# Cross attention on one core: the last batch's right sums for product 4 placed ahead of block 12, and the first loads cut into smaller transfers

## The chip, the core and the metric

The kernel runs on one core of one Trainium2 chip. A core has five engines that run their own instruction streams side by side: TensorE (PE in the profile; its weight loads are listed apart as PEld), VectorE (DVE), ScalarE (ACT), GpSimd (POOL) and SyncE (SP), and 16 DMA engines that move data between HBM and the on-chip memory. SP, ACT and POOL can issue DMA transfers; "SPq" and "ACTq" in a profile row mean such an issue. The metric is device microseconds of one execution. Lower is better.

## The reference

There are 8 batches. All data are float32.

```python
q = jnp.einsum('bcn,dc->bnd', x1, Wq) + bq
k = jnp.einsum('bcn,dc->bdn', x2, Wk) + bk[:, None]
v = jnp.einsum('bcn,dc->bdn', x2, Wv) + bv[:, None]
attn = jax.nn.softmax(jnp.einsum('bnd,bdm->bnm', q, k), axis=2)
attn_out = jnp.einsum('bcm,bnm->bcn', v, attn)
return attn_out + x1
```

x1 and x2 are 8 x 512 x 1024 (batch, channel, position), Wq and Wk are 64 x 512, Wv is 512 x 512.

## The kernel before

The value projection is moved behind the attention. For each batch the kernel makes scores from queries and keys, takes exponentials e (positions m of x2 on the partitions, positions n of x1 along the row), forms y = x2 e, scales each column n by one over the sum of its exponentials, multiplies Wv y, and adds the bias and x1.

Both large products, y = x2 e (the first stage, banks ya and yc) and Wv y (the second stage, banks oa and oc), are cut into 2 x 2 blocks and done with seven block products in place of eight, in the manner of Strassen and Winograd. The table `MULT` (L298) names the operands of each: left blocks and left sums (S1 to S4, made from blocks of x2 or of Wv) and right blocks and right sums (T1 to T4, made from blocks of e or of y). Result block 12 comes out of product 3, block 22 out of 7 and 5, block 21 out of 4 and 6 on top of the bank of 7, block 11 out of 1 and 2. In the last batch products 2, 3, 4 and 7 of the first stage are themselves cut once more into seven products of half the size. `inner_left` (L349) and `inner_right` (L358) make the four left and four right sums for this; `multiply_onto` (L422) runs the seven half-size products, copies partial results from PSUM with ACT into tiles d and v, and `complete` (L450 to L453) adds v onto d on DVE.

`multiply_3` (L475) returns `evict`, called `evict_3`: `complete` (one DVE addition, L452), then two DVE additions (L483) that write block 12 of y from bank a and d. `multiply_4` (L456) starts with the half-size product 1, which needs blocks of e and x2 alone; its second step, half-size product 7, needs T3, one of the sums of `inner_right(s, 4, s.t["T4"], "eT2")`. These sums appear in the profile as eI4eT at L367, four additions of 128 x 512. `evict_y` (L490) has two steps: step 1 adds a PSUM bank and a partial result (L502), step 2 multiplies with one over the sum (L505, L507). `evict_o` (L509) adds bias and x1 to a block of the result and stores it; in the last batch its DVE work is at L526, L534 and L538.

The order on each engine is the order of the program: the whole kernel runs under `manual_schedule`, and nothing reorders it. `head` (L609) prepares batch 0, and `period(s, n, nn, nnn)` (L708) does the products of batch s with the scores of batch n between them. In the last batch n is None: no work of another batch stands between its products. Batches 2 to 5 and the last take the branch `seven`, in which product 7 is cut further too; of these only the last has no next batch.

In `head`, ten warm-up products of 128 x 128 (L635) run on TensorE while the first data come. ACT issues one transfer of Wq and Wk together (`wqk`, 256 KB, L630). SP issues, in this order: x1's channel tiles 0 and 1, then 2 and 3, of columns 0 to 511 (half 0; 512 KB each, L623); eight transfers of x2, 256 KB each (L644), the left 256 columns of each half for the four channel tiles and then the right ones; half 1 of x1 (L623); four blocks of x2 transposed (`load_a`, L133); Wv (L99). TensorE takes the queries of half 0 (L586, 8 products), the left keys (L601, tile ps_kc), the first tile of the right keys (ps_ka), and then the first scores.

Transfers of the hardware queues take their completion semaphores in turn from a ring of eight, common to SP and ACT. A transfer that comes after eight others waits on its issuing engine until the one eight before it has landed.

Of the kernel before, what the change touches and what calls it, by code (L numbers as in the profile page):

```python
# [15 lines left out]
def kernel(  # L16
# [47 lines left out]
    nc = tc.nc  # L64
    P = 128
    B, C, N = x1.shape
    D = wqk.shape[3]
    CT = C // P
    H = 512
# [16 lines left out]
    wqk_sb = const.tile([P, 2, CT, D], F32, name="wqk_sb")  # L86
# [9 lines left out]
    def load_values():  # L96
        for r in range(2):
            for k in range(2):
                nc.sync.dma_start(w[f"{r + 1}{k + 1}"], wvT[r, k])  # L99
# [28 lines left out]
    def load_a(s, *ks):  # L128
        for k in ks:
            s.a[k] = sb.tile(  # L130
                [P, MH, C // 2], F32, tag=f"a{k}", name=f"a{k}_{s.b}", bufs=1 + (k[0] == "2")
            )
            nc.sync.dma_start(s.a[k], x2T[s.b, int(k[0]) - 1, int(k[1]) - 1])  # L133
# [79 lines left out]
    def fold_halves(s, h, op):  # L213
        f = s.mx[h]
        nc.vector.tensor_tensor(f[:, 0, :], f[:, 0, :], f[:, 1, :], op)  # L215

    def highest(s, h, halves=True):
        if halves:
            fold_halves(s, h, ALU.max)
        s.top[h] = sb.tile([P, H], F32, tag="top", name=f"top_{s.b}_{h}", bufs=2)  # L220
        nc.gpsimd.partition_all_reduce(s.top[h], s.mx[h][:, 0, :], P, ReduceOp.max)  # L221
# [136 lines left out]
    def inner_right(s, i, x, *tags):  # L358

        v = {  # L360
            f"{q + 1}{r + 1}": x[:, ts(q, MH // 2), ts(r, H // 2)] for q in range(2) for r in range(2)
        }
        shape = [P, 4 // len(tags), MH // 2, H // 2]
        sums = [sb.tile(shape, F32, tag=t, name=f"eI{i}{t}_{s.b}") for t in tags]
        for z, (k, x, y, op) in enumerate(RIGHT):
            v[k] = sums[z // shape[1]][:, z % shape[1]]
            nc.vector.tensor_tensor(v[k], v[x], v[y], op)  # L367
        s.inner[i, "t"] = v
# [206 lines left out]
    def head_queries(s, x_sb, h, bank=None):  # L575


        if bank:
            ps = ps_a.tile([P, H], F32, tag=bank, name=f"ps_q_{s.b}_{h}")
        else:  # L580
            ps = ps_s.tile([P, 2, H], F32, tag="sc", name=f"ps_q_{s.b}_{h}")[:, 0, :]

        def add(*tiles):
            for c in tiles:
                for r in (lo, hi):
                    nc.tensor.matmul(  # L586
                        ps[r, :], wq_sb[:, c, :], x_sb[:, c, ts(h, H)], start=(c == 0), stop=(c == CT - 1)
                    )
            if c == CT - 1:
                nc.scalar.activation(s.q[:, ts(h, H)], ps, AF.Identity, bias=bq_sb)  # L590

        return add

    def head_keys(s, n, bank):

        ps = ps_a.tile([P, H], F32, tag=bank, name=f"ps_k{bank}_{s.b}")

        def add(*tiles):
            for c in tiles:
                for h, r in ((0, lo), (1, hi)):  # L600
                    nc.tensor.matmul(  # L601
                        ps[r, n], wk_sb[:, c, :], s.x[:, c, ts(h, H)][:, n], start=(c == 0), stop=(c == CT - 1)
                    )
            if c == CT - 1:
                nc.scalar.activation(s.k[:, n], ps[:, n], AF.Identity, bias=bk_sb)

        return add

    def head(s):  # L609

        s.q = sb.tile([P, N], F32, tag="q", name=f"q_{s.b}", bufs=2)
        s.k = sb.tile([P, H], F32, tag="k", name=f"k_{s.b}", bufs=2)
        x1_sb = sb.tile([P, CT, N], F32, tag="x", name="x1_head")
        x2_sb = sb.tile([P, 2, MH, H], F32, tag="e1", name="x2_head")
        s.x = x2_sb.rearrange("p a (b t) n -> p (a b) (t n)", t=2)  # L620

        def load_x1(c, h):
            nc.sync.dma_start(  # L623
                x1_sb[:, c : c + 2, ts(h, H)],
                x1[s.b, c * P : (c + 2) * P, ts(h, H)].rearrange("(t p) n -> p t n", p=P),
            )

        nc.gpsimd.dma_start(bqk_sb, bqk)
        nc.gpsimd.dma_start(bv_sb, bv)
        nc.scalar.dma_start(wqk_sb, wqk)  # L630
        warm = const.tile([P, P], F32, name="warm")
        nc.vector.memset(warm, 0.0)
        ps = ps_a.tile([P, H], F32, tag="a0", name="ps_warm")
        for _ in range(WARM):
            nc.tensor.matmul(ps[:, 0:P], warm, warm, start=True, stop=True)  # L635
        load_x1(0, 0)
        load_x1(2, 0)
        for n in HALVES:
            for c in range(CT):
                to, of = (  # L640
                    x.rearrange("p (h n) -> p h n", h=2)[:, :, n]
                    for x in (s.x[:, c, :], x2[s.b, ts(c, P), :])
                )
                nc.sync.dma_start(to, of)  # L644
        nc.scalar.activation(warm[:, 0:1], warm[:, 0:1], AF.Exp)
        load_x1(0, 1)
        load_x1(2, 1)
        load_a(s, "21", "22", "11", "12")
        load_values()
        tiles = range(CT)  # L650
        head_queries(s, x1_sb, 0, "c1")(*tiles)
        head_keys(s, left, "c0")(*tiles)
        more_keys = head_keys(s, right, "a0")
        more_keys(0)
        s.mx[0] = f = sb.tile([P, 2, H], F32, tag="fold", name=f"max_{s.b}_0", bufs=2)
        copies = [scores(s, 0, i) for i in range(2)]
        for g in range(2):
            nc.scalar.copy(s.e[0][:, g, 0, :], copies[0].ps[g])
            nc.vector.tensor_tensor(f[:, g, :], s.e[0][:, g, 0, :], copies[1].ps[g], ALU.max)
        fold_halves(s, 0, ALU.max)  # L660
        more_keys(*tiles[1:])
        copies[1]()
        more_queries = head_queries(s, x1_sb, 1)
        more_queries(0)
        for i, bank in ((2, "a"), (3, "c")):
            copy = scores(s, 0, i, bank)
            for g in range(2):
                nc.vector.tensor_tensor(f[:, 0, :], f[:, 0, :], copy.ps[g], ALU.max)
            copy()
        highest(s, 0, halves=False)  # L670
        sum_a(s, "S1", "S2")
        more_queries(*tiles[1:])
        load_x(states[1], x1)
        copies = [scores(s, 1, 0), scores(s, 1, 1), scores(s, 1, 2, "c")]
        for g in range(2):
            for i in range(MH):
                first_exponentials(s, g, i)
        for copy in copies:
            copy()
        fold(s, 0, 1, "sum", ALU.add)  # L680
        fold(s, 0, 2, "sum", ALU.add)
        fold(s, 1, 1, "max", ALU.max)
        fold(s, 0, 3, "sum", ALU.add)
# [24 lines left out]
    def period(s, n, nn, nnn):  # L708
# [54 lines left out]
        def add_exponential(i):  # L763
            exponential(n, 0, i)
            add_tile(n, 0, i)
# [20 lines left out]
        if seven:  # L786
            hooks = [{}, {}]
            if n:
                for i in range(MH):
                    lower(n, 0, i)  # L790
                hooks = [
                    {
                        1: lambda: copy_first(n, 0),
                        6: lambda: add_exponential(1),
                        5: lambda: add_exponential(2),
                    },
                    {6: lambda: add_exponential(3)},
                ]
            first(5, (lambda: exponential(n, 0, 0)) if n else None)
            inner_right(s, 3, s.t["22"], "eT1")  # L800
            inner_left(s, 4, s.a["22"], "a12")
            add_7 = multiply_7(s, hooks[0])
            add_7()
            evict_3 = multiply_3(s, hooks[1])
            evict_y(s, "22", (1,))
            evict_3()
            inner_right(s, 4, s.t["T4"], "eT2")
        else:
            first(5)
            if s.b == 0:  # L810
                inner_right(s, 3, s.t["22"], "eT1")
                for i in range(MH):
                    lower(n, 0, i)
            else:
                for i in range(MH):
                    exponentials(n, 0, i)
                start_sum(n, 0)
                inner_right(s, 3, s.t["22"], "eT1")
            first(7)
            if s.b > 1:  # L820
                inner_right(s, 4, s.t["T4"], "eT2")
            evict_3 = multiply_3(s, {})
            if s.b:
                evict_y(s, "22", (1,))
                evict_3()
            else:
                evict_3()
                evict_y(s, "22", (1,))
# [105 lines left out]
```

## Time and profile before

| what | value |
|---|---|
| median of 3 runs | 693.46 us (693.18 to 695.86) |
| profiled execution | 693.62 us |
| its span, first to last instruction | 691.8 us |
| PE busy | 682.8 us, 99% of the span |
| DVE busy | 628.9 us, 91% |
| ACT busy | 276.1 us, 40% |
| POOL busy | 193.5 us, 28% |
| share of the chain that ended last | PE 93%, DMA 3%, DVE 1%, SP's queue 1%, ACT 1% |
| granted TensorE clock | 1.000 |
| transfers issued by SP for x_head (x1, x2 of batch 0) | 4 of 512 KB, 8 of 256 KB; 6.3 and 6.5 us from issue to landing (median) |

In a row of a timeline the first number is the start in us from the span's start, the second the length, then come engine, line, operation, and the tiles as out<-in; a bracket at the end tells how long the engine stood idle before and what released it. A matmul row counts several passes of one instruction, and their ends are modelled. In a row of the chain that ended last, the numbers are start and length of a step that the end of the run hung on.

### The profile page before, as it was taken

What the parts mean: (1) busy time and instruction counts of PE and PEld (TensorE: products, weight loads), DVE (VectorE), ACT (ScalarE), POOL (GpSimd) and SP (SyncE); (2) the same over time, 40 slices, a digit from 0 to 9 for tenths busy, and PEclk for the clock granted to TensorE, in tenths of its full rate; (3) what the DMA queues carried; (4) which work ended last, traced back from release to release, by engine and by line L of the source; (5) the groups of instructions that cost most, each with busy time, mean ns of one, the idle gap of its engine ahead of it and who ended that gap; (6) DMA issues with size and microseconds to landing.
All of it is one profiled execution on the core that took longest, in us unless ns stands there. A gap on an engine that the chain in (4) does not pass through costs nothing.

```text
span 691.8 us, 6647 instructions
## 1 busy us (share of the span) xinstructions
PE 682.8 (99%) x2248; PEld 364.2 (53%) x2248; DVE 628.9 (91%) x809; ACT 276.1 (40%) x439; POOL 193.5 (28%) x147
## 2 busy tenths in 40 slices
PE   9999999999999999999999999999999999999997
PEld 5333554535545565455644566454754545545753
DVE  1999999988999889998999989999799988999785
ACT  2733353146233552345432454424544245243220
POOL 0123113522423223242142321623223232323000
PEclk9999999999999999999999999999999999999999
DMA  9676256954569754786628867198642864268303
GB/s 304 258 214 238 65 182 130 255 161 79 183 114 235 199 106 153 150 231 181 135 111 180 230 181 187 42 198 215 167 92 38 207 166 76 62 148 223 87 0 122
DMA packets 44723, 109.05 MB, mean 158 GB/s; under 512 B 4880, under 2 KB 7184, under 8 KB 44688
## 3 DMA queue, kind: packets, MB, share of 16 engines
q1 hardware_dynamic: 25856, 70.13, 30.1%
q0 software_dynamic: 17424, 36.25, 29.7%
q10 hardware_dynamic: 1408, 2.23, 1.0%
q8 instruction: 18, 0.29, 0.2%
q14 instruction: 17, 0.14, 0.1%
HBM read 72.62 MB, written 16.81 MB: 129 GB/s over the span
## 4 chain that ended last, share of the span: by engine, by line
PE 93%; DMA 3%; DVE 1%; SPq 1%; ACT 1%; issue 0%; DVEq 0%
PE ps_ya L321 24%; PE ps_i L374 17%; PE ps_oa L321 16%; PE ps_oc L321 12%; PE ps_s L191 6%; PE ps_yc L374 5%; PE ps_q L149 4%; PE ps_k L149 3%; PE ps_yc L321 3%; PE ps_ya L374 3%; DMA a<-in_x2T_dram 1%; DMA x_in_x_dram<-in_x_dram 1%; DMA x_head<-in_x_dram 1%; PE ps_sc L191 1%; PE ps_sa L191 1%; DVE aS L110 0%
## 5 line engine op out<-in xcount | busy, mean ns | idle before, releaser
L321 PE MATMUL ps_ya<-eT,aS 128*128 128x512 f32 x256 | 113.1, 595 | 0.0
L332 ACT COPY uy<-ps_ya 128x512 f32<-128x512 f32 x48 | 28.1, 588 | 139.6 <-PE ps_ya L321 126.7
L249 DVE TENSOR_TENSOR e<-e,top 128x1024 f32<-128x1024 f32 x60 | 70.5, 1228 | 11.0 <-POOL top L221 11.0
L321 PEld LDWEIGHTS ps_ya<-eT,aS 128*128 128x128 f32 x256 | 48.0, 190 | 60.9 <-issue 58.5
L253 ACT ACTIVATE e<-e 128x1024 f32<-128x1024 f32 x60 | 62.9, 1059 | 38.6 <-DVE e L249 37.1
L221 POOL PARTITION_ALL_REDUCE top<-max x16 | 32.8, 2052 | 150.8 <-DVE max L215 78.9
L226 POOL PARTITION_ALL_REDUCE den<-sum x16 | 63.4, 3961 | 40.8 <-DVE sum L215 35.8
L321 PE MATMUL ps_oa<-yT,w_S 128*128 128x512 f32 x128 | 57.6, 593 | 0.0
L321 PE MATMUL ps_oc<-y,w 128*128 128x512 f32 x128 | 57.6, 593 | 0.0
L321 PE MATMUL ps_ya<-e,a 128*128 128x512 f32 x128 | 56.3, 593 | 0.3 <-ACT e L244 0.3
L200 ACT COPY e<-ps_s 128x1024 f32<-128x1024 f32 x46 | 45.7, 1027 | 19.3 <-PE ps_s L191 17.5
L332 ACT COPY uo<-ps_oa 128x512 f32<-128x512 f32 x48 | 27.6, 584 | 54.2 <-PE ps_oa L321 44.9
L383 ACT COPY d<-ps_i 128x256 f32<-128x256 f32 x84 | 29.3, 374 | 47.7 <-PE ps_i L374 47.2
L191 PE MATMUL ps_s<-q,k 64*128 64x512 f32 x188 | 47.3, 608 | 0.8 <-ACT q L590 0.8
L551 POOL DMA_DIRECT2D uo<-in_x_dram x21 | 24.9, 1186 | 79.2 <-DVE uo L548 79.2
L555 POOL DMA_DIRECT2D sum<-e x21 | 25.7, 1222 | 66.5 <-DMA sum<-e 37.0
L321 PEld LDWEIGHTS ps_ya<-e,a 128*128 128x128 f32 x128 | 24.2, 190 | 31.3 <-issue 29.6
L321 PEld LDWEIGHTS ps_oa<-yT,w_S 128*128 128x128 f32 x128 | 24.2, 190 | 30.8 <-issue 29.9
L321 PEld LDWEIGHTS ps_oc<-y,w 128*128 128x128 f32 x128 | 24.1, 190 | 31.0 <-issue 28.9
L211 DVE TENSOR_TENSOR max<-max,e 128x1024 f32<-128x1024 f32 x30 | 36.8, 1225 | 3.0
L507 DVE TENSOR_TENSOR y<-y,den 128x512 f32<-128x512 f32 x54 | 33.8, 683 | 0.0
L238 POOL DMA_DIRECT2D den<-row x16 | 8.9, 557 | 79.0 <-DMA row<-few 73.2
(142 smaller groups left out, 1291.4 us busy)
## 6 DMA issues: line engine op xcount, KB each, us to landing
x_in_x_dram<-in_x_dram SPq DMA_DIRECT2D x60, 512.0 KB, 5.9
a<-in_x2T_dram SPq DMA_DIRECT2D x32, 512.0 KB, 7.1
sum<-e POOLq DMA_DIRECT2D x21, 512.0 KB, 5.2
uo<-in_x_dram POOLq DMA_DIRECT2D x21, 512.0 KB, 6.5
out_dram<-uo SPq DMA_DIRECT2D x21, 512.0 KB, 5.1
eT<-eT POOLq DMA_DIRECT2D x12, 512.0 KB, 6.5
den<-row POOLq DMA_DIRECT2D x16, 256.0 KB, 3.6
r<-in_x_dram POOLq DMA_DIRECT2D x7, 512.0 KB, 8.6
```

The source lines that it names most:

```text
L149: nc.tensor.matmul(ps[r, :], w_sb[:, c, :], s.x[:, c, ts(h, H)], start=(c == 0), stop=(c == CT - 1),)
L191: nc.tensor.matmul(ps[g], s.k[r, ts(i, P)], s.q[r, ts(h, H)], start=True, stop=True)
L200: nc.scalar.copy(e[:, :, i, :], whole)
L211: nc.vector.tensor_tensor(f, e[:, :, 0, :] if i == 1 else f, e[:, :, i, :], op)
L221: nc.gpsimd.partition_all_reduce(s.top[h], s.mx[h][:, 0, :], P, ReduceOp.max)
L226: nc.gpsimd.partition_all_reduce(s.den[h], s.mx[h][:, 0, :], P, ReduceOp.add)
L249: nc.vector.tensor_tensor(e, e, top, ALU.subtract)
L253: nc.scalar.activation(e, e, AF.Exp)
L321: nc.tensor.matmul(ps[:, n], left[ka][:, k, ts(j, P)], right[kb][:, k, n], start=opens and k == 0, stop=i in (2, 3, 4) and k == n_k - 1, s ...
L332: nc.scalar.copy(s.tmp[i][:, j, :], ps)
L374: nc.tensor.matmul(ps, s.inner[i][ka][:, k, :], s.inner[i, "t"][kb][:, k, :], start=opens and k == 0, stop=z in (2, 3, 4) and k == MH // 2 ...
L507: nc.vector.tensor_tensor(y[:, j, :], y[:, j, :], rden, ALU.mult)
```

## The change

Two places change. In `period`, within the branch `seven`, the last batch (n is None) now makes the right sums of product 4 before the eviction of block 12, and the other batches keep the order that they had. In `head`, the transfer of Wq and Wk becomes two, Wq first, and half 0 of x1 comes in four transfers of one channel tile (256 KB) in place of two of two tiles. Half 1 of x1 is loaded as before; its helper function is written out in place.

```diff
-        nc.scalar.dma_start(wqk_sb, wqk)
+        for i in range(2):
+            nc.scalar.dma_start(wqk_sb[:, i], wqk[:, i])
...
-        load_x1(0, 0)
-        load_x1(2, 0)
+        for c in range(CT):
+            nc.sync.dma_start(x1_sb[:, c, 0:H], x1[s.b, ts(c, P), 0:H])
...
-        load_x1(0, 1)
-        load_x1(2, 1)
+        for c in (0, 2):
+            nc.sync.dma_start(
+                x1_sb[:, c : c + 2, ts(1, H)],
+                x1[s.b, c * P : (c + 2) * P, ts(1, H)].rearrange("(t p) n -> p t n", p=P),
+            )
...
             evict_3 = multiply_3(s, hooks[1])
             evict_y(s, "22", (1,))
-            evict_3()
+            if n:
+                evict_3()
             inner_right(s, 4, s.t["T4"], "eT2")
+            if not n:
+                evict_3()
```

More of the change, by code (lines that the diff above doesn't have):

```diff
@@ L620, in head @@
         s.x = x2_sb.rearrange("p a (b t) n -> p (a b) (t n)", t=2)
[L622 to L626, printed above, removed]
         nc.gpsimd.dma_start(bqk_sb, bqk)
         nc.gpsimd.dma_start(bv_sb, bv)
-        nc.scalar.dma_start(wqk_sb, wqk)
+        for i in range(2):
+            nc.scalar.dma_start(wqk_sb[:, i], wqk[:, i])
         warm = const.tile([P, P], F32, name="warm")
```

## The prediction

> **What bounds the kernel now.** I read the page's busy table first, then the chain that ended last at both ends of the run, then the timelines of those two places, because the change touches only the first 10 us and the last batch.
>
> The page, first line of its busy table, and one line of the table of windows (us; busy time and count of PE, PEld, DVE, ACT, POOL; clock, DMA share, GB/s):
>
> ```profile
> PE 682.8 (99%) x2248; PEld 364.2 (53%) x2248; DVE 628.9 (91%) x809; ACT 276.1 (40%) x439; POOL 193.5 (28%) x147
> ...
> 25.00:650.00 625.00, 624.49 (x2024) 331.75 (x2025) 589.88 (x752) 260.32 (x409) 189.40 (x140) 1.00 0.63 158
> ```
>
> PE is the bound, and from 25 to 650 us it stands still for 0.5 us in all. Whatever makes PE start its dense stretch earlier, or removes a hole near the end, goes to the end one for one; nothing else counts. The holes lie in the head and in the last batch.
>
> The chain in the last batch (start us, us, what), then the timelines of DVE and PE there:
>
> ```profile
> 653.81 0.66 ACT d L383 x2
> ...
> 654.49 0.70 DVE d L452
> ...
> 655.90 0.68 DVE y L483
> 656.58 0.61 DVE eI4eT L367
> ...
> 657.21 1.30 DVE eI4eT L367 x2
> ...
> 658.65 1.97 PE ps_i L374 x8
> ```
>
> ```profile
> 652.31 1.01 DVE L502 TENSOR_TENSOR y<-ps_yc,uy 128x512 f32<-128x512 f32 x2
> 654.49 0.69 DVE L452 TENSOR_TENSOR d<-d,v 128x512 f32<-128x512 f32 x1 [1.16 <-ACT d L383]
> 655.29 1.29 DVE L483 TENSOR_TENSOR y<-ps_ya,d 128x512 f32<-128x512 f32 x2
> 656.49 0.68 DVE L367 TENSOR_TENSOR eI4eT<-eT 128x512 f32<-128x512 f32 x1
> ...
> 655.34 1.03 PE L374 MATMUL ps_i<-eT,a 128*128 128x256 f32 x4
> 658.65 1.97 PE L374 MATMUL ps_i<-eI4eT,aI 128*128 128x256 f32 x8 [2.28 <-DVE eI4eT L367]
> ```
>
> The reader is to see that PE has done the first step of product 4 by 656.4 and then waits for its right sums (eI4eT), that these stand on DVE behind the eviction of block 12 (L452, L483), and that this eviction itself waited 1.16 us for ACT while DVE had nothing to do.
>
> In the head, PE's timeline and SP's waits:
>
> ```profile
> 1.04 4.62 PE L635 MATMUL ps_warm<-warm 128*128 128x128 f32 x20 [1.04 <-DVE warm L632]
> 5.90 3.65 PE L586 MATMUL ps_q<-x_head,wqk_sb 128*64 128x512 f32 x16 [0.23 <-DMA x_head<-in_x_dram]
> 9.35 1.96 PE L601 MATMUL ps_kc<-x_head,wqk_sb 128*64 128x256 f32 x16
> 11.50 0.65 PE L601 MATMUL ps_ka<-x_head,wqk_sb 128*64 128x256 f32 x4 [0.19 <-DMA x_head<-in_x_dram]
> ...
> SPq L133 <- DMA x_head<-in_x_dram: 1.6, 4, 0.4
> ```
>
> The queries start 0.23 us after the warm-up ends, and the keys' fourth tile is taken when it lands (PEld waits for it until 10.65).
>
> **Part 1, the tail.** Nothing is added or removed; four DVE additions (L367) move ahead of evict_3 (one L452, two L483).
>
> When the sums can run. Their operand T4 was issued by POOL at 635.8 and took at most 10.6 us, so it is there by 646.4; their tile eT2 was last read by product 6, over by 643.4. So they follow the y22 additions, which end at 653.32; DVE starts an independent operation some 0.07 before the reported end of the one ahead (656.49 after an end at 656.58), so at 653.25. At the measured spacing (starts 656.49, 657.21, 657.82, 658.42, next operation 659.02) the third starts 1.33 later and lasts 0.68: T3, the one that product 4's second step needs, is there at 655.26, and with the 0.14 us of issue seen ahead of 658.65, PE may go at 655.4.
>
> What PE gains. The first step starts at 655.34 and its four passes take 0.86 (the spacing of the steps around it), so the second starts at 656.20 instead of 658.65: **2.45 us**. The wait reads 2.28 because the page counts from a modelled end.
>
> What is late next. The sums hold DVE for 2.53 (656.49 to 659.02), so evict_3 starts at 655.78 instead of 654.49, 1.29 later, and with its 2.00 ends at 657.78. What follows on DVE began at 659.02 and now begins at 657.78: 1.24 earlier, the idle time filled. PE is 2.45 earlier and DVE only 1.24, so every cover behind shrinks by 1.2:
> - second-stage product 1 (PE at 663.90 - 2.45 = 661.45) needs two scalings of y11 (657.78 + 1.25 = 659.0) and bank a, read by evict_3 until 657.8. Covered.
> - product 6 (667.33 - 2.45 = 664.88) needs yT2, which ended at 665.17, now 663.93. 0.95 left.
> - product 2 (670.77 - 2.45 = 668.32) needs y21's halves, done at 668.52 and 669.19, now 667.28 and 667.95; the second is read two passes (0.43) later. 0.8 left.
> - products 7 and 4 need T3 and T4 (670.33 and 671.46, now 669.1 and 670.2); PE reaches 7 at 675.2. Covered.
> - ACT's copy of product 4's v reuses the buffer that L452 reads, until 656.47 now; PE has the value only at 657.2. Nothing behind it on ACT is held.
> - The stores: SP and ACT issue each when its rows are done, and they move with PE. The 3.7 us from the last matmul (688.1) to 691.8 stay.
>
> So -2.45. If a cover failed, DVE's own shift of 1.24 is the least that remains; I take the full value, as the narrowest cover (0.8) is wide against the 0.14 of one hand-over.
>
> **Part 2, the head.** One more transfer on ACT's queue, two more on SP's; the bytes are the same. SP shows that a transfer waits for the landing of the one eight before it (x2's tiles, a and w all wait for earlier x_head tiles), so three more shorten what is in flight.
>
> PE: the queries cannot start before the warm-up ends (5.66), so they gain at most 5.90 - 5.66 = 0.24. Then the keys of the left half: steps of 0.43, the fourth ready to run at 10.39 instead of 10.65. But its tile was issued at 4.15 and landed 6.5 us later, at 10.6, and it stands behind the same 2.25 MB as before. So the 0.24 is lost there: **0**. From the keys on everything hangs together: scores, maxima (L668 until 20.53), POOL's maximum (20.63 to 23.31), first subtraction 23.57, first PE product 24.96.
>
> DMA: the engines are full from 3 us on (share 1.02 and 1.05 in windows 3 to 5.5 and 7 to 10.75). Wq and Wk go as rows of 1 KB instead of 2 KB; in the trace a 1 KB packet takes 46 ns and a 2 KB one 84, so 256 x 46 - 128 x 84 = 1.0 us over 16 engines, +0.06. SP's issues: the four x1 tiles cost at most 0.45 each as the double ones did, plus 0.05, so x2's first two are out by 4.4; its third and fourth wait for Wq and x1's first tile, which cannot land later than the double transfers did (5.45 and 5.76). Issued by some 6.9 for a turn that comes at 10.6: hidden by the line ahead.
>
> Bounds. Best: the keys' tile comes earlier (the window 6.25 to 7.00 moved 205 GB/s against 355 after it, 0.3 us of bytes, which could vanish), and then PE's 0.24 is the most that can be used: -0.24. Worst of cost per transfer: x1's other half lands 1.36 apart for 512 KB, x2's tiles 0.74 for 256 KB, so a split costs at most 2 x 0.74 - 1.36 = 0.12, three cost +0.36. I take +0.06, the packets' own.
>
> [...]
>
> **Sum.** 693.62 (the profiled execution; span 691.8) - 2.45 + 0.06 = 691.23. That execution lies 0.16 above the median of 693.46, so in medians 691.1.
>
> **Rivals.**
> - A. A cover fails: PE waits at product 2 or 6 because DVE came only 1.24 forward. For it: covers of 0.8 and 0.95 in place of 2 us. Against: each still lies above the hand-over. At worst 1.24 remains: 692.3.
> - B. The head gains: x2's left tiles come sooner. For: the dip at 6.25 to 7.00. Against: it falls where x2's first packets and the small bias transfers run, and neither moves. 690.8.
> - C. The sums do not run early, since something else holds them: then only the head's +0.06 stays, 693.5. Against: both operands are there 7 us before.
> - D. Other side: the shorter flight starves the head. Place: SP holding x2's fourth left tile until x1's first has landed. If the four small tiles landed together at 7.34, as the second double did, and the tile still took 6.5 from its issue, it would land at 13.9, 3.25 late: 694.4. It decides above 2.4 late. Against: those 6.5 us are queueing, which shrinks as issue is later.
>
> **How the numbers follow.** Forecast (tail in full, head within -0.1 and +0.36) 0.66, A 0.12, B 0.12, C 0.04, D 0.06. The range takes in A and B and the scatter of the runs shown (0.3 below the median): 690.4 to 692.6. 0.5% is 3.5 us, about what a measurement here can tell from no change: the forecast, A, B and C lie inside it. Faster than that needs 1.0 us more than forecast, 0.09, mostly B with scatter; slower needs D at its worst, 0.04; within 0.87.
>
> **What would show it.** In the profile after: the PE wait for eI4eT gone and the four L367 of eI4eT from 653.3 on, relative to an unchanged stretch; evict_3 directly behind them without a wait for ACT; second-stage products back to back. In the head: queries from 5.66, the keys' fourth tile still awaited, about 10.7, and the first product at about 25.0. Wrong if PE waits for y or yT in the second stage, or if the first product moves by more than 0.4.

## The result and the profile after

| | before | after |
|---|---|---|
| median | 693.54 us (693.17 to 695.86, 6 runs) | 691.27 us (690.85 to 691.72, 6 runs) |
| profiled execution | 693.62 us | 690.85 us |
| its span | 691.8 us | 689.1 us |

The ratio of after to before is 0.9951, with a 95% interval of 0.9932 to 0.9969 (the two medians alone give 0.9967; that of before depends on which of its six runs came out short). The forecast of 691.1 us is 0.17 us off. It called the change too small to be told from none, though, with a chance of 0.87, and the interval leaves 1 out. The executions after lie within 0.9 us of each other; those before spread over 2.7 us.

The first line of the busy table of the page of after, and the longest waits of PE in it (engine, tile and line, what was waited for, us in total, times, longest):

```profile
PE 682.3 (99%) x2248; PEld 364.0 (53%) x2248; DVE 630.0 (91%) x809; ACT 275.8 (40%) x439; POOL 190.5 (28%) x147
```

```profile
PE ps_warm L630 <- DVE warm L627: 1.0, 1, 1.0
PE ps_s L191 <- ACT q L590: 0.8, 1, 0.8
PE ps_ya L321 <- ACT e L244: 0.3, 1, 0.3
```

The wait for eI4eT, 2.3 us and the longest of before, is gone. The timelines of PE and DVE in the last batch of after:

```profile
654.80 1.03 PE L374 MATMUL ps_i<-eT,a 128*128 128x256 f32 x4
655.66 1.89 PE L374 MATMUL ps_i<-eI4eT,aI 128*128 128x256 f32 x8
...
660.84 3.60 PE L321 MATMUL ps_oa<-y,w 128*128 128x512 f32 x8
664.27 3.60 PE L321 MATMUL ps_oa<-yT,w_S 128*128 128x512 f32 x8
667.71 3.60 PE L321 MATMUL ps_oc<-y,w 128*128 128x512 f32 x8
```

```profile
652.71 0.68 DVE L367 TENSOR_TENSOR eI4eT<-eT 128x512 f32<-128x512 f32 x1
...
654.03 0.68 DVE L367 TENSOR_TENSOR eI4eT<-eT 128x512 f32<-128x512 f32 x1
654.63 0.68 DVE L367 TENSOR_TENSOR eI4eT<-eT,eI4eT 128x512 f32<-128x512 f32 x1
655.23 0.69 DVE L452 TENSOR_TENSOR d<-d,v 128x512 f32<-128x512 f32 x1
656.02 1.29 DVE L483 TENSOR_TENSOR y<-ps_ya,d 128x512 f32<-128x512 f32 x2
657.23 3.09 DVE L507 TENSOR_TENSOR y<-y,den 128x512 f32<-128x512 f32 x5
...
662.16 1.23 DVE L262 TENSOR_TENSOR yT<-yT,y 128x1024 f32<-128x1024 f32 x1
...
666.97 0.41 DVE L505 TENSOR_TENSOR y<-uy,den 128x256 f32<-128x256 f32 x1
```

The second step of product 4 follows the first by 0.86 us, the length of its four passes. The sums stand ahead of block 12 (L452, L483), no operation shown has a bracket, and the second-stage products follow each other by 3.43.

In the head, the timeline of PE in after, and below it one row of before; the last row of each is the first product of the dense stretch:

```profile
1.04 4.63 PE L630 MATMUL ps_warm<-warm 128*128 128x128 f32 x20 [1.04 <-DVE warm L627]
5.61 3.65 PE L586 MATMUL ps_q<-x_head,wqk_sb 128*64 128x512 f32 x16
9.09 1.90 PE L601 MATMUL ps_kc<-x_head,wqk_sb 128*64 128x256 f32 x16
11.08 0.65 PE L601 MATMUL ps_ka<-x_head,wqk_sb 128*64 128x256 f32 x4
...
24.54 7.13 PE L321 MATMUL ps_ya<-e,a 128*128 128x512 f32 x16 [0.31 <-ACT e L244]
```

```profile
24.96 7.13 PE L321 MATMUL ps_ya<-e,a 128*128 128x512 f32 x16 [0.31 <-ACT e L244]
```

So the two profiled executions differ in four places: 2.45 us in the tail; 0.42 in the head (24.96 to 24.54, as x2's fourth left tile landed at 10.21 instead of 10.61 and the tile behind it, the first right one, at 10.95 instead of 11.37); 0.16 more at the keys of batch 1, which waited for a load; and 0.29 the other way at the end, where the time from the landing of the last store to the start of the last instruction grew from 0.87 to 1.16. 693.62 - 2.45 - 0.42 - 0.16 + 0.29 = 690.88, against 690.85 measured.

### The profile page after: what moved, and what is told of

Read it like the earlier page. It is cut to its first block, busy times and chain, and to the rows that moved or that the text cites. A ratio compares the mean times of both kernels' runs of the same rounds, so it can differ in the third digit from the quotient of the medians.

```text
span 689.1 us, 6652 instructions
## 1 busy us (share of the span) xinstructions
PE 682.3 (99%) x2248; PEld 364.0 (53%) x2248; DVE 630.0 (91%) x809; ACT 275.8 (40%) x439; POOL 190.5 (28%) x147
## 4 chain that ended last, share of the span: by engine, by line
PE 94%; DMA 4%; ACT 1%; DVE 1%; SPq 0%; issue 0%; DVEq 0%; ACTq 0%
PE ps_ya L321 24%; PE ps_i L374 17%; PE ps_oa L321 16%; PE ps_oc L321 12%; PE ps_s L191 6%; PE ps_yc L374 5%; PE ps_q L149 4%; PE ps_k L149 3%; PE ps_ya L374 3%; PE ps_yc L321 3%; DMA a<-in_x2T_dram 1%; DMA x_in_x_dram<-in_x_dram 1%; PE ps_sc L191 1%; PE ps_sa L191 1%; DMA x_head<-in_x_dram 1%; DMA wqk_sb<-in_wqk_dram 1%
## 5 line engine op out<-in xcount | busy, mean ns | idle before, releaser
L226 POOL PARTITION_ALL_REDUCE den<-sum x16 | 60.4, 3775 | 40.8 <-DVE sum L215 35.8
L548 DVE SCALAR_TENSOR_TENSOR uo<-ps_oc,bv_sb,uo 128x512 f32<-128x512 f32 x42 | 29.5, 741 | 1.5 <-PE ps_oc L321 1.5
```

The lines of the kernel that those rows point to most:

```text
L226: nc.gpsimd.partition_all_reduce(s.den[h], s.mx[h][:, 0, :], P, ReduceOp.add)
```

## The experiments

Three questions were open: whether the 2.45 us are the moved sums alone; whether the 0.42 of the head belong to the change, and to which half of it; and why the executions before spread so much more. For the head there were two theories, that x1's smaller transfers do it or that the split of Wq and Wk does, and the rival that it is chance. None of the kernels leaves a part of the computation out. e5, e6 and e9 add work whose result nothing uses.

**e1: the moved sums alone.**

```diff
             evict_y(s, "22", (1,))
-            evict_3()
+            if n:
+                evict_3()
             inner_right(s, 4, s.t["T4"], "eT2")
+            if not n:
+                evict_3()
```

> The moved sums alone; all loads as before. Theory (the sums' place on DVE made the wait): PE's wait of 2.28 us for eI4eT is gone, product 4's second step follows its first by 0.86 us, the span is 2.4 to 2.5 us shorter than before's 691.8, and the first product of the first stage (ps_ya) still starts at about 24.95. Rival (part of the 2.7 us by which the changed kernel's span is shorter comes from elsewhere in the last batch, such as the stores): the span falls by a different amount, and the shift behind product 4 isn't constant.

Measured: 690.88 us (690.70 to 691.29, 5 runs); before, run beside it, 694.31 (692.93 to 698.05, 29 runs); ratio 0.9954 (0.9942 to 0.9966). The first product starts at 24.94, as before (24.96), and the wait is gone. The last store lands 0.86 us ahead of the last instruction. These lines alone gain as much as the changed kernel, as far as these runs can tell.

**e2: the loads alone.**

```diff
-        nc.scalar.dma_start(wqk_sb, wqk)
+        for i in range(2):
+            nc.scalar.dma_start(wqk_sb[:, i], wqk[:, i])
...
-        load_x1(0, 0)
-        load_x1(2, 0)
+        for c in range(CT):
+            nc.sync.dma_start(x1_sb[:, c, 0:H], x1[s.b, ts(c, P), 0:H])
```

> The smaller first transfers alone; the sums stay behind block 12. Theory (the head is earlier by itself): queries start at 5.6, ps_ya at about 24.55 instead of 24.96, PE's wait for eI4eT stays at 2.3 us, and the end of the last product moves by -0.4 to -0.6 us. Of that some 0.3 us is lost behind the last store, because the three extra transfers turn the ring of completion semaphores, so that the last store's one stands in the middle of the list that SP walks at the end and not near its end: span -0.1 to -0.3. Rival (chance): ps_ya starts at 24.9 to 25.0, and the span is equal within 0.1.

Measured: 695.35 us (693.19 to 697.49, 12 runs), ratio 1.0010 (0.9997 to 1.0024). The same loads that in after came 0.4 earlier came 1.2 later here: x2's fourth left tile landed at 11.79. The timeline of PE in e2, the head:

```profile
5.18 1.94 PE L586 MATMUL ps_q<-x_head,wqk_sb 128*64 128x512 f32 x8
8.14 1.94 PE L586 MATMUL ps_q<-x_head,wqk_sb 128*64 128x512 f32 x8 [1.02 <-DMA x_head<-in_x_dram]
...
12.68 0.65 PE L601 MATMUL ps_ka<-x_head,wqk_sb 128*64 128x256 f32 x4 [0.19 <-DMA x_head<-in_x_dram]
```

x1's third tile landed at 8.09, where in after it landed at 6.36, and everything behind it is late.

This profile also showed something else. In the traces the granted clock changes only at borders that lie 3.41 us apart, counted from its first rise: in e2 at 4.65, 660.01 and 663.43, and 660.01 - 4.65 is 192 times 3.413. The timeline of PE in e2 at product 4, and the windows of three such stretches there (columns as in the prediction: busy time and count of PE, PEld, DVE, ACT, POOL; granted clock, DMA share, GB/s):

```profile
659.70 3.45 PE L374 MATMUL ps_i<-eI4eT,aI 128*128 128x256 f32 x8 [2.28 <-DVE eI4eT L367]
662.95 1.27 PE L374 MATMUL ps_yc<-eT,a 128*128 128x256 f32 x4
```

```profile
656.60:660.01 3.41, 1.13 (x6) 0.70 (x5) 3.38 (x6) 0.37 (x1) 0.00 (x0) 1.00 0.01 2
660.01:663.43 3.42, 3.42 (x10) 2.70 (x9) 3.42 (x8) 0.61 (x2) 0.00 (x0) 0.50 0.00 0
663.43:666.84 3.41, 3.41 (x17) 3.02 (x16) 3.38 (x6) 0.78 (x3) 0.00 (x0) 1.00 0.00 0
```

The eight passes that took 1.97 in before take 3.45. In the stretch before that, PE stood still for 2.28 us; then the clock was granted at 0.50 for one stretch. Half the clock for 3.41 us costs up to 1.7. This became the theory for the spread of before: the wait of 2.28 us sometimes costs a second time.

**e3: Wq and Wk in two transfers, alone.**

```diff
-        nc.scalar.dma_start(wqk_sb, wqk)
+        for i in range(2):
+            nc.scalar.dma_start(wqk_sb[:, i], wqk[:, i])
```

> Only Wq and Wk in two transfers; x1 comes in two of 512 KB. Theory A (what counts is that data flow from the start without the pause that before shows from 2.25 to 2.75 us, and that x1's smaller transfers do this): pause still there, third and fourth left tiles of x2 land as before (9.9 and 10.6), queries at about 5.8 (x1's first landing stays 5.8), ps_ya at 24.9 to 25.0. Theory B (the split of the weights does it, by having ACT's transfer begin at once): ps_ya at 24.5 to 24.6, x2's fourth left tile at about 10.2. The end list is turned by one place: some 0.06 us of the closing either way.

Measured: 695.14 us (693.56 to 696.18, 12 runs), ratio 1.0005 (0.9991 to 1.0018). Wq landed at 5.42, no earlier, and the first product started at 24.97. The split does nothing by itself. This profile has the half clock as well, again behind a stretch that held the whole wait (windows of e3):

```profile
655.87:659.28 3.41, 1.13 (x6) 0.74 (x5) 3.38 (x6) 0.37 (x1) 0.00 (x0) 1.00 0.01 2
659.28:662.69 3.41, 3.41 (x10) 2.70 (x9) 3.41 (x8) 0.74 (x2) 0.00 (x0) 0.50 0.00 0
```

**e4: half 0 of x1 in four transfers, alone.**

```diff
-        load_x1(0, 0)
-        load_x1(2, 0)
+        for c in range(CT):
+            nc.sync.dma_start(x1_sb[:, c, 0:H], x1[s.b, ts(c, P), 0:H])
```

> Only x1's half 0 in four transfers; Wq and Wk come in one. Theory A: no pause at the start, x2's fourth left tile lands at about 10.2, queries at 5.6, ps_ya at 24.5 to 24.6. Theory B: as before, ps_ya at 24.9 to 25.0 and the pause is there. If the pause is chance, neither this run nor the one with the split weights follows its theory.

Measured: 694.40 us (693.51 to 696.13, 12 runs), ratio 1.0012 (1.0001 to 1.0023), just above 1. x1's first tile landed at 4.13, the queries started at 5.31, and still x2's fourth left tile landed at 10.96 and the first product started at 25.31, 0.35 later than before. The windows of before, after and e4 from 2 to 3 us, one fence each:

```profile
2.00:3.00 1.00, 1.00 (x7) 1.00 (x6) 0.00 (x0) 0.55 (x1) 0.48 (x1) 1.00 0.63 49
```

```profile
2.00:3.00 1.00, 1.00 (x7) 1.00 (x6) 0.00 (x0) 0.99 (x1) 0.47 (x1) 1.00 0.89 288
```

```profile
2.00:3.00 1.00, 1.00 (x7) 1.00 (x6) 0.00 (x0) 0.52 (x1) 0.47 (x1) 1.00 0.85 287
```

The smaller x1 transfers do what one of the theories said: data flow at 287 GB/s in a time in which the double ones move 49. But the advantage is gone by the time that counts: from 5 to 6 us e4 moves 234 GB/s, and before 396. What PE waits for stands behind 2.25 MB, and those were not there sooner.

**e5: the wait filled with products that nothing uses.** Before, with five products of 128 x 256 between the first and the second step of product 4 in the last batch.

```diff
             inner_product(s, i, z, *steps[z])
+            if z == 1 and i == 4 and s.b == B - 1:
+                for _ in range(5):
+                    nc.tensor.matmul(third, s.inner[i]["11"][:, 0, :],
+                                     s.inner[i, "t"]["11"][:, 0, :], start=True,
+                                     stop=True, skip_group_check=True)
```

> Before, with five products of 128 x 256 that nothing uses (0.43 us each, 2.15 in all) put on PE between product 4's first and second step, where PE waits 2.28 us for its sums. Theory (the wait sometimes halves PE's clock: the trace has the granted clock at 0.5 for one stretch of 3.41 us right behind the wait in two of the runs of part of the change, none in the others): the wait stays, the sums come no earlier, but all executions lie together at 693.2 to 693.8, with none at 695, and the profile has no half clock in the last batch. Rival (the scatter of 2 us between executions comes from the loads at the start): executions still fall on both 693.4 and 695.2 in about equal numbers.

Measured: 693.79 us (693.07 to 696.10, 12 runs; 11 of them at most 694.41); before, run beside it, 695.00 (693.37 to 696.14, 23 runs). The timeline of PE in e5:

```profile
655.49 1.03 PE L374 MATMUL ps_i<-eT,a 128*128 128x256 f32 x4
656.35 2.32 PE L449 MATMUL ps_i<-eT,a 128*128 128x256 f32 x10
658.71 1.99 PE L374 MATMUL ps_i<-eI4eT,aI 128*128 128x256 f32 x8
```

The second step starts where it did, 658.71, so nothing was won by time; but none of the 12 runs has a mean clock under 0.999, where 10 of the 23 of before have 0.998 or less. The median falls by 1.2 us with work added. The ratio, 0.9994 (0.9983 to 1.0005), does not exclude 1, since the medians of before jump between two groups; the clocks are what tells, and they say that the standstill is the cause of the half clock. The one execution at 696.10 has a mean clock of 0.999, so it was slow for another reason, which was not found.

**e6: the wait made longer.** Before, with one addition of 128 x 1024 on DVE ahead of the sums.

```diff
             evict_3()
+            if not n:
+                nc.vector.tensor_tensor(s.t["12"][:, 0:2], s.t["T4"][:, 0:2], s.t["T4"][:, 0:2], ALU.add)
             inner_right(s, 4, s.t["T4"], "eT2")
```

> Before, with one more addition of 128 x 1024 (1.22 us) on DVE between block 12's eviction and the right sums: PE's wait grows from 2.28 to 3.5 us. Theory (a wait of this length halves the clock whenever it fills most of one stretch of 3.41 us): nearly every execution has the half clock, so they lie together near 693.4 + 1.22 + 1.6 = 696.2, few below 695. Rival (the length of the wait doesn't matter for the clock): both groups move by 1.22, to 694.6 and 696.4, and keep their shares.

Measured: 696.41 us (694.25 to 698.33, 12 runs), ratio 1.0023 (1.0010 to 1.0036). Ten of the 12 have a mean clock of 0.998 or less (median 696.5), four of them 0.995 and 697.2 to 698.3; two have 0.999 or more and took 694.25 and 694.75. What the four lost beside one half-clock stretch was not traced. The profiled one is of the two. Its wait reads 3.4 us, and its windows show why it kept the clock:

```profile
654.37:657.78 3.41, 1.50 (x7) 0.96 (x6) 3.31 (x5) 0.37 (x1) 0.00 (x0) 1.00 0.01 2
657.78:661.20 3.42, 1.91 (x9) 1.74 (x10) 3.38 (x7) 0.37 (x1) 0.00 (x0) 1.00 0.00 0
```

The wait fell across the border of two stretches, 1.91 us in one and 1.51 in the other, and neither was followed by a drop. So, in these profiles, the threshold lies between 1.91 and 2.28 us of standstill within one stretch.

**e7: the changed kernel again.** No edit.

> The changed kernel once more, beside before and the next one. Theory: no wait, so no half clock in the last batch, executions at 690.8 to 691.8; ps_ya starts between 24.5 and 25.5 as the loads fall. Rival for the head (the smaller transfers do make it start earlier): ps_ya again at 24.5 to 24.6.

Measured: 691.18 us (690.55 to 692.38, 6 runs), ratio 0.9955 (0.9940 to 0.9969). The first product started some 0.35 earlier than before, and the last store landed 1.16 ahead of the last instruction, both as in after.

**e8: as many transfers as make the ring of eight come round.** The changed kernel puts three transfers more on the ring than before; e8 adds five more.

```diff
-        for c in (0, 2):
-            nc.sync.dma_start(
...
+        for c in range(CT):
+            nc.sync.dma_start(x1_sb[:, c, ts(1, H)], x1[s.b, ts(c, P), ts(1, H)])
...
-                nc.sync.dma_start(w[f"{r + 1}{k + 1}"], wvT[r, k])
+                if r == k == 0:
+                    nc.sync.dma_start(w["11"], wvT[0, 0])
+                else:
+                    for i in range(2):
+                        nc.sync.dma_start(w[f"{r + 1}{k + 1}"][:, i], wvT[r, k][:, i])
```

> The changed kernel with five transfers more in the head (half 1 of x1 in four, three of the four blocks of Wv in two each), eight more than before in all, so the last store has the completion semaphore that it had before. Theory (the closing is longer by 0.3 us in the changed kernel because SP walks its list of semaphores after the last store landed): from that landing to the end 0.87 us as before, not 1.16, and the median 0.2 to 0.4 below the changed kernel's of this call. Rival (the closing depends on the moment, not on the ring): 1.1 to 1.2 us, median equal within 0.1.

Measured: 691.42 us (690.47 to 692.04, 6 runs), ratio 0.9956 (0.9941 to 0.9970). The end is as in the kernel before: the last store lands 0.86 ahead of the last instruction. The median is no lower than the changed kernel's, where 0.2 to 0.4 less was expected; in the profiled execution x2's fourth left tile landed at 10.97, which took more than the 0.3 back.

**e9: DVE made later by 2.44 us.** The changed kernel, with two additions of 128 x 1024 behind the moved evict_3, to see how much the covers of the prediction's first part are worth.

```diff
             if not n:
                 evict_3()
+                nc.vector.tensor_tensor(s.t["12"][:, 0:2], s.t["T4"][:, 0:2], s.t["T4"][:, 0:2], ALU.add)
+                nc.vector.tensor_tensor(s.t["12"][:, 0:2], s.t["T4"][:, 0:2], s.t["T4"][:, 0:2], ALU.add)
```

> The changed kernel with two more additions of 128 x 1024 on DVE (2.44 us) right behind block 12's eviction in the last batch. Theory (behind the moved sums DVE has 0.7 to 0.9 us in hand before PE must wait for it): PE waits about 1.7 us at second-stage product 6 for yT, and at most 0.1 more at product 2, so the span is 1.7 to 1.9 longer than the changed kernel's (689.1 and 689.3 in its two profiles) and the median about 693.0; a wait of 1.7 us is too short for the half clock (waits whose part within one stretch of 3.41 us was 1.9 or less went without it), so no execution lies a further 1.5 up. Rival A (DVE has 2.4 us or more in hand): no wait, median 691.2. Rival B (DVE sets the pace there already): the full 2.44, median 693.6.

Measured: 693.00 us (692.40 to 693.80, 10 runs), ratio 0.9981 (0.9971 to 0.9991). The timeline of PE in e9:

```profile
667.14 3.67 PE L321 MATMUL ps_oa<-yT,w_S 128*128 128x512 f32 x8 [1.49 <-DVE yT L262]
```

The wait came at product 6, where the prediction put one of its two narrow covers. PE lost 1.7 us there for 2.44 us of work, so DVE had about 0.75 in hand. None of the ten runs has a clock under 0.999: a standstill of 1.5 us does not bring it down.

**e10: the moved sums alone, again.** Edit as in e1.

> The moved sums alone, once more, to set beside the changed kernel's executions (690.55 to 692.38). Theory (the smaller first transfers bring nothing on the whole: they cost 0.3 us in the closing, and the landing of x2's left tiles scatters as widely or more): median 690.8 to 691.1, 0.2 to 0.4 below the changed kernel's 691.2, and less spread. Rival (the head's 0.4 us earlier start is worth its closing): median 691.2 or more.

Measured: 691.07 us (690.65 to 693.83, 9 runs), ratio 0.9960 (0.9947 to 0.9974). With e1 the moved sums alone have 14 runs with a median of 691.06; the changed kernel, with e7, has 12 with 691.25. The new loads bring nothing that these runs can tell, and a small cost is not shown either.

**e11 and e12: without the transfer of the value bias in the head.** In e2 and e9, where x1's third tile landed at 8.0 to 8.1, the bias of the values, 2 KB on POOL's queue, landed shortly ahead of it (the traces have it as 16 packets of 128 bytes, not as 128 of 16). e11 is the changed kernel and e12 the moved sums alone, each with this transfer moved to the end of `head`.

```diff
-        nc.gpsimd.dma_start(bv_sb, bv)
...
         fold(s, 0, 3, "sum", ALU.add)
+        nc.gpsimd.dma_start(bv_sb, bv)
```

> The changed kernel with the transfer of the value bias (128 packets of 16 bytes on POOL's queue, issued at 1.93) moved to the end of the head. With x1 in 256 KB transfers, x2's fourth left tile landed between 10.21 and 11.8 in six profiles; where it was late, x1's third tile had landed together with this bias transfer, at 8.0 to 8.1 in place of 6.4. Theory that the small packets of the bias hold the start-up up: x1's third tile lands at 6.3 to 6.5 and x2's fourth left tile at 10.0 to 10.4, the first product starts at 24.3 to 24.7, and the median falls below the changed kernel's 691.25 to 690.8 to 691.0, with no execution over 691.7. Rival, that the bias transfer is only late with the others and holds nothing up: landings scatter as before (10.2 to 11.8), median 691.1 to 691.4, highest 692 or more.

> The moved sums alone (x1 in 512 KB as before the change) with the transfer of the value bias moved to the end of the head. In this arrangement x2's fourth left tile landed at 10.37 to 10.65, a narrow band. Theory that the small packets hold the start-up up: it gains what they take at most, x2's fourth left tile at 10.2 to 10.4, median 690.8 to 691.0 against 691.06. Rival: 10.4 to 10.65, median 691.0 to 691.2. If this one is the lower of the two kernels of this call, the smaller transfers of the head bring nothing even without the bias.

Measured: e11 690.99 us (690.36 to 691.72, 6 runs), ratio 0.9945 (0.9931 to 0.9959); e12 691.30 (690.60 to 693.10, 6 runs), ratio 0.9955 (0.9937 to 0.9973). The timeline of PE in e11:

```profile
12.04 0.65 PE L601 MATMUL ps_ka<-x_head,wqk_sb 128*64 128x256 f32 x4 [0.20 <-DMA x_head<-in_x_dram]
...
25.50 7.13 PE L321 MATMUL ps_ya<-e,a 128*128 128x512 f32 x16 [0.31 <-ACT e L244]
```

x1's third tile landed at 7.48 and x2's fourth left tile at 11.14, with no bias transfer near. So the bias transfer is not needed for a late landing, and for x1 in 256 KB this theory falls. The medians, 690.99 and 691.30, lie on either side of the earlier ones by amounts that six runs can't tell from nothing. In e12, with x1 in double transfers, the tile landed at 10.20, which the theory had expected; that is one profile, and whether the bias plays a part there stays open.

## Why the prediction was right and where it was wrong

**Part 1, the tail: right, step by step.** In the trace of after, product 4's first step starts 0.54 earlier than before, so 0.54 is added to compare. The first sum starts at 652.71 + 0.54 = 653.25 (worked out: 653.25); evict_3 at 655.77 (655.78); what follows it at 657.77 (657.78); product 4's second step at 656.20 (656.20). The narrow covers read 664.27 - 663.39 = 0.88 (0.95) and 667.71 + 0.43 - 667.38 = 0.76 (0.8), and e9 found 0.75 in hand by loading them until they failed. Rival A is out, and so is C.

Part of the closeness of the time is luck: the profiled pair gained 0.58 us that the forecast did not have (0.42 in the head, 0.16 at batch 1's keys) and lost 0.29 at the end, which it did not have either.

**The term that was missing.** The step that failed is "How the numbers follow": it took the saving from one profiled execution, and took the 2.7 us between the runs shown for scatter ("0.5% is 3.5 us, about what a measurement here can tell from no change"). The measured interval reaches 0.0018 to either side, which is 1.3 us, so the 2.4 us that it forecast could already be told. And the executions of before are of two kinds. Before ran 83 times beside the experiments. In 36 of those the mean clock is 0.998 or less, with a median of 695.23; in 47 it is 0.999 or more, with 693.61, and the median of all is 694.92. Half the clock for one stretch of 3.41 us in 694 makes 0.9975. The same wait thus costs some 1.6 us more in 43 executions of 100. e5 shows the cause: with the wait filled, the low clocks are gone. And of the 54 executions that have the moved sums (after, e1 and e7 to e12), none has a clock under 0.999. Where the low clock lies is seen in e2 and e3, which keep the wait; no profile of before itself caught it. The clock is not all of the spread: eight of the 47 took 695.2 to 695.9 with their clock kept, and with the moved sums single ones took up to 693.83 (e10). What these lost is open.

The profiled execution of before was one in which the wait was split (windows of before):

```profile
654.05:657.47 3.42, 2.31 (x11) 1.70 (x9) 2.84 (x5) 0.78 (x3) 0.00 (x0) 1.00 0.01 2
657.47:660.88 3.41, 2.23 (x11) 2.01 (x11) 3.41 (x7) 0.60 (x2) 0.00 (x0) 1.00 0.00 0
```

PE stood still for 1.11 and 1.18 us in the two stretches. Against this execution the sum for the tail was right, and the forecast time came close with it, for the time after has no such lottery. The saving over all executions, 694.92 to 691.25, is 3.7 us, and 2.4 against those with the clock kept. The 695.86 among the three runs shown was the hint, though its clock is not on record.

The shares fit a simple count. If the border of the stretches falls anywhere with the same chance, a wait of 2.28 us puts at least T of itself into one stretch with the chance (3.41 + 2.28 - 2T) / 3.41; 0.43 gives T = 2.1, an estimate, between the 1.91 and 2.28 that the profiles show. For e6's 3.4 us this T leaves (4.2 - 3.41) / 3.41 = 23% without a drop; 2 of 12 were seen.

The Trainium skill, "TensorE: Matmul & The Clock Gate", has the stretch in Part 1: a window of 3413 ns that runs freely. The traces agree: the half clock in e2 and e3 lasted 3.41 us. Its section "Why this matters for your kernels" advises no idle gaps of more than about 3 us. Here 2.28 us were enough, so on this point the measurement decides: it is what falls within one window that counts, and two thirds of it idle suffice.

**Part 2, the head: the bounds were too narrow.** The prediction put 0 for the queries and 0.06 for the packets, and bounds of -0.24 to +0.36. After gained 0.42, e7 some 0.35; but the same loads lost 1.2 in e2, and x1's smaller transfers by themselves 0.35 in e4. By the prediction's own sign ("if the first product moves by more than 0.4") it was wrong here, just. The landing of x2's fourth left tile says it best: with x1 in 512 KB it came at 10.20 to 10.65 in before, e1, e3, e5, e6, e10 and e12, on the mean at 10.48; with x1 in 256 KB at 10.21 to 11.79 in after, e2, e4, e7, e8, e9 and e11, on the mean at 10.99. So the statement that this tile "stands behind the same 2.25 MB" did not make it land alike: seven profiles of each kind have it 0.5 later with the smaller transfers, while the medians of the executions (691.25 against 691.06) show no such cost.

The best case stopped at the 0.23 ahead of the queries and left out the wait of 0.19 for the first right tile (ps_ka), which the prediction's own row shows. PE's start hangs on that tile in these profiles: ps_ka starts 0.13 behind its landing in before (11.37, 11.50) and in after (10.95, 11.08), and 0.14 behind it in e2 (12.54, 12.68). From before to after the landing moved by 0.42, and so did the first product. The worst case priced transfers by what they cost in a steady flow, where this is the start of one.

The start of PE also moves by the clock. In e3 the passes of the warm-up products follow each other by 0.21 until 3.9 and by 0.11 from there; the ten products took 3.85, in e2 4.21, in before 4.62 and in after 4.63. The clock rose between 3.9 and 7.2 us in the profiles, at 5.52 in before and 5.56 in after, so that these two don't differ by it; but in e5 it rose at 7.0, and the left keys started at 9.92 instead of 9.35 though x1 and x2 had landed as in before. Its first product came at 25.27, 0.31 later.

Rival D named the price of a late x1 tile, though it expected 3.25 us and by another way; in e2 1.2 of it is there. Rival B is what the profile of after shows, and the part runs show that it is not what the change does each time. Why x1's third tile lands at 6.4 to 6.7 in some executions and at 7.5 to 8.1 in others was not found; e11 shows it at 7.48 without the transfer of the value bias.

**The closing.** "The 3.7 us from the last matmul (688.1) to 691.8 stay" failed by 0.29. At the end SP goes through a list of semaphores, and the part of the list that lies behind the last store's is still to be done when it lands: nothing in before, five entries 0.06 us apart in after. With three transfers more, the last store takes another place on the ring of eight and so another place in the list. e1, with no transfer added, has 0.86; e4, with two, 1.24; e8, with eight, 0.86 again, which shows that it is the place and not the number.

## What to carry to other kernels

A wait of PE is worth its own length and, where two thirds of a 3.4 us stretch can fall into it, a clock that is halved for the next stretch: read the granted clock behind every wait of 2 us or more, and compare several executions before one profile is taken for the kernel. When executions fall into two groups, ask what is different in them before it is called scatter. Here smaller first transfers started the flow sooner, but the tile that PE waits for, behind the same bytes, did not on the mean come sooner for it.

## What the runs showed of the hardware that was not expected

- A standstill of 2.28 us of PE inside one stretch of 3.41 us was followed by half the granted clock in the next (e2, e3); 1.91 and 1.51 (e6) and 1.79 (e4) in a stretch were not.
- The first transfers behave otherwise than later ones: from 2 to 3 us the kernels with x1 in 512 KB moved 35 to 102 GB/s (before, e1, e3, e5, e6, e10, e12), those with 256 KB 252 to 303 (after, e2, e4, e7, e8, e9, e11). By the time of x2's fourth left tile nothing was left of it: it landed at 10.48 and 10.99 on the mean.
- The number of transfers in a program moves its end by up to 0.4 us, by the ring position of the last store (from its landing to the last instruction 0.86 and 0.87 in before, e1 and e8, against 1.16 in after, 1.24 in e4 and 1.29 in e3).
